# A transformer block's prelude dealt anew: the re-ordered bias rows copied by ScalarE, their transposes a later word

## The chip, the cores and the metric

The kernel runs on one core of a Trainium2 chip. The metric is the time of one execution on the device in microseconds (us). One core has TensorE (PE, its weight loads are shown as PEld), VectorE (DVE), ScalarE (ACT), GpSimd (POOL) and SyncE (SP, which here only issues transfers). Each works through its own list of instructions in order.

## The reference, cut to what matters

A PixArt-like block for 16 sequences of 256 tokens, width 256, 16 heads of 16, context of 256 tokens:

```
c_proj = silu(c) @ W_mod + b_mod          # shift_a, scale_a, gate_a, shift_m, scale_m, gate_m
x_norm = ln(x) * (1 + scale_a) + shift_a
q, k, v = split(x_norm @ W_qkv + b_qkv)
x = x + gate_a * (softmax(q k^T / 4) v @ W_proj + b_proj)
q_c = ln(x) @ W_qc + b_qc ;  k_c, v_c = split(ln(context) @ W_kvc + b_kvc)
x = x + softmax(q_c k_c^T / 4) v_c @ W_cproj + b_cproj
x = x + gate_m * (gelu((ln(x)*(1+scale_m)+shift_m) @ W_mlp1 + b_mlp1) @ W_mlp2 + b_mlp2)
```

All of it is float32; most products are done as three products of a rounded high part and a low part (hi·hi, hi·lo, lo·hi).

## The kernel before, in words

The attention work is cut into 32 units: self-attention ("s") and cross-attention ("c") of each sequence. A unit has 8 pairs of heads. While unit n is in its 8 beats (score tiles turned with the exponential, then the output product), the score maxima of unit n+1 and the projections of units n+2 and n+3 run beside it, by a written plan. Stage −1 is the 8 beats before unit 0, in which only unit 0's score maxima (its S tiles, from `s_tile`, reduced by VectorE into `mx`) are made. The MLP comes last.

Ahead of stage −1 stands the prelude, which this change deals with. Its order is a string of words, `E_['PRE']`; each word calls one function that issues instructions on one or several engines, and every engine keeps the order in which they were issued. `E_['SL']` has further words that are put behind a beat: key (−1, 3) is beat 3 of stage −1. So moving a word moves all its instructions, and its DMAs, past what other words put on the same engine.

The words that matter here:

- `load` issues the loads of x and of the first weights (wm0 and wm1 are shift_a's and scale_a's columns of W_mod, wk, wq, wv those of W_qkv; in the trace all are called wf). `lg`, `lp`, `lc`, `wm`, `ld2`, `ld3` are later loads.
- `b12`, `b5` and the like: so many zero matmuls (`busy`, wz by wz into the bank s0); each is two passes of 128x128 in the trace.
- `silu`, `turn`: silu of the condition, turned by two transposes into sT. `brow`: the bias rows (32 rows of 128) turned into columns bT, and their re-ordered copy bp, whose odd and even columns are turned as well. `scale`, `shift`: shift_a and scale_a by 16-wide products of sT with wm1, wm0 into st, then cpT by VectorE; `sc1` adds 1. `bk`, `bq`, `bv`: the biases of k, q, v, again 16-wide.
- `L0a`, `L0b`, `L0d`: layer norm of unit 0's x (statistics, rstd by GpSimd, normalising into xn); `T0t`, `T0h`, `T0l`: its transposes, high part xTh by ScalarE, low part xTl by VectorE. 1 and 2 in their place are units 1 and 2; `T2p` makes the low part by GpSimd.
- `hik`, `lok` and so on: high part (ScalarE) and low part (GpSimd, for v VectorE) of a weight.
- `K0a`, `K0m`: the two halves of unit 0's k product; `K0h`, `K0l`: its high and low part; `K0x`, `K0y`, `K0w`: the transfers of high, high again and low into big, from which the S tiles read. Q and unit 1 likewise. A `p` at the end of such a transfer's name puts it on GpSimd's queue instead of SyncE's. An S tile of a unit needs all six transfers.
- `z0kp` and so on: GpSimd fills a half of big with zeros. `vone`, `gs`, `M0`, `ga`, `pb`: ones beside v, gate products, the first turned maxima.

Of the kernel before, what the change touches and what calls it, by code (L numbers as in the profile page):

```python
# [10 lines left out]
F32 = mybir.dt.float32  # L11
# [5 lines left out]
P = 128  # L17
# [4 lines left out]
def pixart_block(  # L22
# [29 lines left out]
                return tc.keep_in_program_order(i) if self.on else i  # L52
            return issue

    E_ = {'CUT': 8, 'LN': {'s': 'pool', 'c': 'pool', 'q': 'pool'}, 'ON': (1, 1, 1), 'L0': -16, 'L1': 1, 'S0': -7, 'A0': 0, 'T0': 1, 'S1': 5, 'A1': 7, 'L2': 9, 'T1': 9, 'S2': 32, 'AP': 23, 'DV': (0, 1), 'HP': (1, 0), 'BZ': {}, 'AV': {1: [(1, 2), (1, 3)], 9: [(0, 0), (0, 1)]}, 'AHEAD': (0, 0, 0, 0, 0, 2), 'TW': {(21, 6): 'cb', (23, 5): 'u0', (23, 7): 'u1', (25, 2): 'u2', (27, 3): 'u3', (27, 7): 'h2a', (28, 0): 'l2 h0p u5', (28, 2): 'h1p', (28, 4): 'h3p', (28, 7): 'u4 u6', (29, 0): 'l3d', (29, 1): 'l0', (29, 2): 'l1', (29, 7): 'h5p', (30, 1): 'u7 h6d h7p', (30, 3): 'h4p', (31, 1): 'l4 l6d', (31, 2): 'l5d x2', (31, 4): 'l7', (31, 7): 'b2'}, 'BE': 'G0 av P g0 A1 G1 G2 N1 F7 g1 S0 PF s2 G3 aT aL p2 a2 G4 x3 b3 S1 S2 T2 C r0 G5 S3 G6 S4 s3 CF x4 F8 g2 G7 S5 F9 p3 S6 G8 a3 r1 G9 F10 G10 T3 g3 b4 S7 s4 F11 S8 S9 F12 G11 p4 a4 F13 r2 S10 G12 x5', 'XP': 1, 'IL': 1, 'MF': 0, 'SH': 4, 'RAMP': 1, 'HA': 1, 'MP': 16, 'W': (7, 1, 0, 0), 'PRE': 'z0kp load L0a z0qp L0b b12 silu hik turn lc lok one0 L0d brow ld2 scale sc1 T0t b5 L1a b1 T0h T0l z1kp L1b shift K0a bk L1d hiq K0m bq lg loq K0h hiv T1t L2a T1h K0l lp T1l Q0a K0yp K0x lov Q0m bv K1a Q0h V0a K1b Q0l K0w Q0yp Q1a Q0x Q1b Q0w K1y ld3 b7 wm V0b L2b Q1l K1l', 'SL': {(-1, 0): 'K1w z1qp L2c', (-1, 1): 'T2t one1 T2h V1a', (-1, 2): 'T2p', (-1, 3): 'z2kp K1xp ga L3a Q1yp V1b', (-1, 4): 'Q1wp pb Q1x vone M0 gs', (-1, 5): 'z2qp', (-1, 6): 'ld4 K2a L3b K2m L3p', (-1, 7): 'L3c cb lx gm', (0, 0): 'mods sp3', (0, 1): 'sp0', (0, 3): 'sp1', (0, 4): 'sc2', (0, 6): 'one2', (1, 1): 'sp2', (1, 2): 'sp4'}}

    PE = InOrder(nc.tensor, True)
    ACT, DVE, POOL, SP = (InOrder(e, True) for e in (nc.scalar, nc.vector, nc.gpsimd, nc.sync))

    const = ctx.enter_context(tc.tile_pool(name="const", bufs=1))  # L60
    work = ctx.enter_context(tc.tile_pool(name="work", bufs=2))
# [18 lines left out]
    ident = const.tile([P, P], F32, name="ident")  # L80
# [14 lines left out]
    BMOD, BQKV, BKVC, BM1 = 0, 12, 20, 24  # L95
# [13 lines left out]
    brow = const.tile([32, P], F32, name="brow")  # L109
# [31 lines left out]
    sp = [psum.tile([P, 512], F32, tag=f"s{r}", name=f"s{r}", bufs=1) for r in range(2)]  # L141
# [44 lines left out]
    def f_turn():  # L186
# [2 lines left out]
            PE.transpose(pst[:, k * B:(k + 1) * B], th[:, k * P:(k + 1) * P], ident[:B, :B])  # L189
        ACT.mul(sT.rearrange("p k b -> p (k b)"), pst[:, :KC * B], 0.5)  # L190

    def f_brow():
        pst = sp[1][:, :96]
        PE.transpose(pst[:, :32], brow, ident[:32, :32])
        ACT.copy(bT[:, 0:32], pst[:, :32])
        odd = pst[:, 32:96].rearrange("p (f r) -> p f r", f=2)
        bp = work.tile([32, 2, 2, 64], F32, tag="A", name="bp", bufs=1)
        DVE.tensor_copy(bp, brow.rearrange("r (c f) -> r f c", f=2).unsqueeze(2).to_broadcast([32, 2, 2, 64]))
        for f in range(2):
            PE.transpose(odd[:, f], bp[:, f].rearrange("r j c -> r (j c)"), ident[:32, :32])  # L200
# [87 lines left out]
    wm = []  # L288
# [9 lines left out]
    gm = []  # L298
# [19 lines left out]
    def layernorm(src, name):  # L318
# [541 lines left out]
    def mlp_T(b):  # L860
# [162 lines left out]
    u0, u1 = units[:2]  # L1023
# [4 lines left out]
    u2 = units[2]  # L1028
# [40 lines left out]
    u3 = units[3]  # L1069
# [3 lines left out]
    for i in range(5):  # L1073
        word[f"sp{i}"] = lambda i=i: f_split(i)
    word["vone"] = lambda: [POOL.memset(v[:, :, :, HD:], 1.0) for v in vts]
    for n, f in (("load", f_load), ("silu", f_silu), ("turn", f_turn), ("brow", f_brow),
                 ("scale", f_scale), ("sc1", f_sc1), ("shift", f_shift),
                 ("lg", f_loads_g), ("lp", f_loads_p), ("lc", f_loads_c), ("lx", f_loads_x),
                 ("ga", f_ga), ("pb", f_pb), ("gs", f_gs), ("cb", f_cb),
                 ("wm", f_wm), ("mods", f_mods), ("sc2", f_sc2), ("gm", f_gm)):  # L1080
        word[n] = f
    for i in range(3):
        for n, f in (("b", f_b), ("hi", f_hi), ("lo", f_lo)):
            word[n + "qkv"[i]] = lambda f=f, i=i: f(i)
# [167 lines left out]
    last, o, q = units[-1], units[-1].post, units[-2].post  # L1252
# [97 lines left out]
```

## Time and profile before

| | us |
|---|---|
| runs | 740.02, 740.80, 744.46; median 740.8 |
| profiled execution | 740.98 |
| its span, first to last instruction | 739.2 |
| TensorE busy | 728.0 (98%) |
| VectorE, ScalarE, GpSimd busy | 586.0, 555.9, 544.9 |
| mean granted TensorE clock | 0.991 of full |

In the profile a row of the timeline has: start, length, engine, line, operation, output<-inputs, shapes, count, and in brackets how long the engine stood idle ahead of it and what ended that. Every instruction has line 51, the helper that records it, so rows are told apart by their tiles. A row of a table by stretches has the stretch, its length, busy time with the number of instructions, the granted TensorE clock, the share of the DMA engines and GB/s.

### The profile page before, as it was taken

How to read it: one execution, taken by the hardware profiler on the slowest of the kernel's cores; microseconds unless marked ns; L12 is line 12 of the kernel's file. 1: busy time of each engine (PE TensorE's matmuls, PEld its weight loads, DVE VectorE, ACT ScalarE, POOL GpSimd, SP SyncE). 2: the span in 40 equal slices, each digit the busy share in tenths (PEclk: the TensorE clock that was granted, in tenths of full speed). 3: DMA queues.
4: the chain of work that ended last, by engine and by line, in shares of the span. 5: the costliest groups of instructions: out<-in, count | busy, mean ns of one | idle time of the engine just before them, and what ended most of it. 6: DMA issues, size and time to landing. Idle time of an engine off the chain costs nothing.

```text
span 739.2 us, 24891 instructions
## 1 busy us (share of the span) xinstructions
PE 728.0 (98%) x10098; PEld 643.5 (87%) x10098; DVE 586.0 (79%) x1218; ACT 555.9 (75%) x963; POOL 544.9 (74%) x572
## 2 busy tenths in 40 slices
PE   7999999999999999999999999999999999999997
PEld 7888888888888888888888888888888999999997
DVE  4778898889898898888889888888835676787872
ACT  2458888888888888888888888899886666556663
POOL 5686769778696876969687898978746767767743
PEclk8989999999999999999999999999999999999999
DMA  5653344333424334332533444344311314334221
GB/s 161 202 175 125 126 147 142 119 128 135 140 94 177 125 119 151 127 137 97 187 118 126 155 151 154 110 154 143 109 60 43 115 51 103 91 95 107 83 61 58
DMA packets 67237, 90.56 MB, mean 123 GB/s; under 512 B 6194, under 2 KB 38740, under 8 KB 67124
## 3 DMA queue, kind: packets, MB, share of 16 engines
q1 hardware_dynamic: 66452, 87.40, 35.6%
q8 instruction: 80, 1.31, 0.8%
q0 software_dynamic: 400, 1.31, 0.5%
q10 hardware_dynamic: 272, 0.26, 0.1%
q14 instruction: 33, 0.27, 0.1%
HBM read 26.97 MB, written 8.46 MB: 48 GB/s over the span
## 4 chain that ended last, share of the span: by engine, by line
PE 94%; POOL 2%; DVE 2%; ACT 1%; issue 1%; POOLq 0%; ACTq 0%
PE s L51 18%; PE o L51 16%; PE st L51 16%; PE ph L51 10%; PE ps_q L51 4%; PE ps_qc L51 4%; PE ps_kc L51 4%; PE ps_v_c L51 3%; PE ps_k L51 3%; PE ps_P_s L51 3%; PE ps_v_s L51 3%; PE ps_P_c L51 2%; PE psT_q L51 1%; PE psA_s L51 1%; PE ps_h L51 1%; PE psA_c L51 1%
## 5 line engine op out<-in xcount | busy, mean ns | idle before, releaser
L51 DVE TENSOR_REDUCE mx<-s 128x2 f32<-128x512 f32 x504 | 324.5, 683 | 65.4 <-PE s L51 59.4
L51 ACT ACTIVATE pt<-st 128x1024 f32<-128x1024 f32 x252 | 258.9, 1027 | 18.6 <-PE st L51 8.7
L51 PE MATMUL s<-big 63*128 63x256 f32 (+1 forms) x1024 | 185.8, 299 | 0.4 <-DVE mx L51 0.2
L51 PEld LDWEIGHTS s<-big 63*128 63x128 f32 (+1 forms) x1024 | 133.9, 186 | 18.9 <-DVE l_kc L51 6.6
L51 PE MATMUL st<-big 64*128 64x256 f32 (+1 forms) x1024 | 134.5, 299 | 0.0
L51 POOL TENSOR_TENSOR hl<-hf,hh 128x512 fp32r<-128x512 f32 x64 | 85.2, 1335 | 54.2 <-ACT hh L51 54.1
L51 PE MATMUL o<-pt,v 128*32 128x256 f32 x2048 | 123.8, 382 | 0.0
L51 PEld LDWEIGHTS st<-big 64*128 64x128 f32 (+1 forms) x1024 | 96.7, 186 | 15.0 <-issue 12.4
L51 PEld LDWEIGHTS o<-pt,v 128*32 128x32 f32 x2048 | 60.0, 109 | 41.5
L51 ACT ACTIVATE hf<-ph,bT 128x256 f32<-128x256 f32 x114 | 47.9, 472 | 33.7 <-PE ph L51 33.7
L51 ACT ACTIVATE hh<-ph,bT 128x256 fp32r<-128x256 f32 x114 | 47.9, 473 | 25.2 <-PE s L51 13.1
L51 ACT COPY oT<-o 128x512 f32<-128x512 f32 x63 | 36.9, 586 | 32.8 <-PE o L51 32.8
L51 PE MATMUL st<-big,hh 128*128 128x256 f32 x256 | 45.3, 277 | 0.0
L51 PE MATMUL s<-big,hh 128*128 128x256 f32 x256 | 45.2, 277 | 0.0
L51 PE MATMUL ph<-wkch,wself 128*128 128x256 f32 x224 | 44.7, 283 | 0.0
L51 PE MATMUL ph<-wqch,wself 128*128 128x256 f32 x224 | 44.6, 283 | 0.0
L51 PE MATMUL ps_k<-xTh_s,wself 64*128 64x256 f32 (+1 forms) x232 | 43.6, 293 | 0.0
L51 PE MATMUL ps_q<-xTh_s,wself 64*128 64x256 f32 (+1 forms) x240 | 41.4, 292 | 0.0
L51 POOL TENSOR_SCALAR xn_c<-c,mv_c,rs_c 128x256 f32<-128x256 f32 x32 | 38.9, 1226 | 1.7
L51 PE MATMUL ps_v_s<-wself,xTh_s 64*128 64x256 f32 x224 | 39.7, 298 | 0.0
L51 PEld LDWEIGHTS st<-big,hh 128*128 128x128 f32 x256 | 38.8, 188 | 0.0
L51 PEld LDWEIGHTS s<-big,hh 128*128 128x128 f32 x256 | 38.8, 188 | 0.0
(254 smaller groups left out, 2504.1 us busy)
## 6 DMA issues: line engine op xcount, KB each, us to landing
big<-h_kc SPq DMA_DIRECT2D x32, 256.0 KB
big<-h_qc SPq DMA_DIRECT2D x32, 256.0 KB
big<-h_k SPq DMA_DIRECT2D x30, 256.0 KB
big<-h_q SPq DMA_DIRECT2D x30, 256.0 KB
big<-l_k SPq DMA_DIRECT2D x16, 256.0 KB
g<-gd SPq DMA_DIRECT2D x16, 256.0 KB
c<-in_ctx_dram SPq DMA_DIRECT2D x16, 256.0 KB
big<-l_kc SPq DMA_DIRECT2D x16, 256.0 KB
```

The lines of the kernel that those rows point to most:

```text
L51: i = f(*a, **k)
```

## The change

The copy bp is a word of its own (`bp`) on ScalarE instead of VectorE; its transposes and what reads them are the word `bro2`, later in the prelude; the four small copies into bT become two wide ones, one on VectorE. The words of the prelude and of stage −1 are in another order. There are 28 zero matmuls instead of 25. Two transfers of unit 1 (low part of k, first copy of the high part of q) go from SyncE's to GpSimd's queue.

```diff
-'PRE': 'z0kp load L0a z0qp L0b b12 silu hik turn lc lok one0 L0d brow ld2 scale sc1 T0t b5 L1a b1 T0h T0l z1kp L1b shift K0a bk L1d hiq K0m bq lg loq K0h hiv T1t L2a T1h K0l lp T1l Q0a K0yp K0x lov Q0m bv K1a Q0h V0a K1b Q0l K0w Q0yp Q1a Q0x Q1b Q0w K1y ld3 b7 wm V0b L2b Q1l K1l',
-'SL': {(-1, 0): 'K1w z1qp L2c', (-1, 1): 'T2t one1 T2h V1a', (-1, 2): 'T2p', (-1, 3): 'z2kp K1xp ga L3a Q1yp V1b', (-1, 4): 'Q1wp pb Q1x vone M0 gs', (-1, 5): 'z2qp', (-1, 6): 'ld4 K2a L3b K2m L3p',
+'PRE': 'load L0a z0kp z0qp L0b silu b15 hik turn L0d brow bp lok T0t lg scale b5 lc sc1 ld2 L1a T0h one0 z1kp bro2 T0l hiv hiq shift K0a L1b bk K0m bq loq K0h b1 L1d K0l Q0a L2a T1t T1h lp K0yp K0x Q0m T1l bv K1a lov Q0h K0w V0a Q0l K1b Q1a L2b Q0x Q1b Q0w Q1l K1y V0b Q0yp b7 K1l ld3',
+'SL': {(-1, 0): 'wm one1 L2c z1qp', (-1, 1): 'T2t T2h V1a', (-1, 2): 'K1wp T2p', (-1, 3): 'ga K1xp L3a Q1yp V1b z2kp', (-1, 4): 'M0 Q1xp Q1wp pb L3b vone gs', (-1, 5): 'z2qp ld4', (-1, 6): 'K2a K2m L3p',
...
+    def f_bp():
+        bp = work.tile([32, 2, 2, 64], F32, tag="A", name="bp", bufs=1)
+        odd_rows.append(bp)
+        ACT.copy(bp, brow.rearrange("r (c f) -> r f c", f=2).unsqueeze(2).to_broadcast([32, 2, 2, 64]))
+
     def f_brow():
-        pst = sp[1][:, :96]
+        pst = sp[1][:, :32]
         PE.transpose(pst[:, :32], brow, ident[:32, :32])
         ACT.copy(bT[:, 0:32], pst[:, :32])
-        odd = pst[:, 32:96].rearrange("p (f r) -> p f r", f=2)
-        bp = work.tile([32, 2, 2, 64], F32, tag="A", name="bp", bufs=1)
-        DVE.tensor_copy(bp, brow.rearrange("r (c f) -> r f c", f=2).unsqueeze(2).to_broadcast([32, 2, 2, 64]))
+
+    def f_bro2():
+        odd = sp[1][:, 32:96].rearrange("p (f r) -> p f r", f=2)
         for f in range(2):
-            PE.transpose(odd[:, f], bp[:, f].rearrange("r j c -> r (j c)"), ident[:32, :32])
+            PE.transpose(odd[:, f], odd_rows[0][:, f].rearrange("r j c -> r (j c)"), ident[:32, :32])
         to = bT[:, 32:40].rearrange("p (g i f) -> p g i f", i=2, f=2)
         for par in range(2):
             rows = slice(64 * par, 64 * par + 64)
-            for g in range(2):
-                r = BQKV + 6 * g + par
-                ACT.copy(to[rows, g], odd[rows, :, r:r + 3:2].rearrange("p f i -> p i f"))
+            src = odd[rows, :, BQKV + par:BQKV + par + 12].rearrange("p f (g s) -> p g s f", g=2)
+            (DVE.tensor_copy, ACT.copy)[par](to[rows], src[:, :, 0:3:2])
```

TensorE's list at the program's start, before (s_110 and s_111 are the banks sp[0] and sp[1]; wf_112 holds wm0 and wm1):

```order
L51 MATMUL s_110<-wz 128x128 x12
L51 MATMUL st<-ident,c_sb 128x16 x2
L51 MATMUL s_111<-ident,brow 128x32
L51 MATMUL s_111<-ident,bp 128x32 x2
L51 MATMUL st<-sT,wf_112 128x16 x4
L51 MATMUL psT_s_185<-ident,xn_s_164 128x128 x4
L51 MATMUL s_110<-wz 128x128 x6
L51 MATMUL st<-sT,wf_112 128x16 x4
L51 MATMUL ps_k_217<-xTh_s_199,wself 128x256
```

And with the change:

```order
L51 MATMUL s_110<-wz 128x128 x15
L51 MATMUL st<-ident,c_sb 128x16 x2
L51 MATMUL s_111<-ident,brow 128x32
L51 MATMUL psT_s_168<-ident,xn_s_160 128x128 x4
L51 MATMUL st<-sT,wf_112 128x16 x4
L51 MATMUL s_110<-wz 128x128 x5
L51 MATMUL s_111<-ident,bp 128x32 x2
L51 MATMUL st<-sT,wf_112 128x16 x4
L51 MATMUL ps_k_217<-xTh_s_197,wself 128x256
```

The transposes of bp moved behind those of xn, the scale product and the zeros; nothing else of the head left it.

GpSimd's list from x_2's reciprocal root to the last transfer of unit 1, before (big_75 is read by unit 0's S tiles, big_76 by unit 1's):

```order
L51 DMA big_75<-h_q_301 32x4x512
L51 TENSOR_SCALAR rs_s_372<-mv_s_369 128x2
L51 TENSOR_TENSOR rs_s_372<-rs_s_372,mhalf 128x2
L51 MEMSET big_76 128x2048
L51 TENSOR_SCALAR xn_s_388<-x_177,mv_s_369,rs_s_372 128x256 x2
L51 TENSOR_TENSOR xTl_s_405<-y_s_420,xTh_s_404 128x512
L51 MEMSET big_77 128x2048
L51 DMA big_76<-h_k_317 32x4x512
L51 DMA big_76<-h_q_339 32x4x512
L51 DMA big_76<-l_q_375 32x4x512
```

And with the change:

```order
L51 TENSOR_SCALAR rs_s_335<-mv_s_332 128x2
L51 TENSOR_TENSOR rs_s_335<-rs_s_335,mhalf 128x2
L51 DMA big_75<-h_q_302 32x4x512
L51 TENSOR_SCALAR xn_s_389<-x_192,mv_s_332,rs_s_335 128x256 x2
L51 MEMSET big_76 128x2048
L51 DMA big_76<-l_k_368 32x4x512
L51 TENSOR_TENSOR xTl_s_405<-y_s_421,xTh_s_404 128x512
L51 DMA big_76<-h_k_322 32x4x512
L51 DMA big_76<-h_q_345 32x4x512
L51 MEMSET big_77 128x2048
L51 DMA big_76<-h_q_345 32x4x512
L51 DMA big_76<-l_q_349 32x4x512
```

Unit 0's second copy of h_q went behind the root, and two transfers of unit 1 came in from SyncE's list.

VectorE's list from the shift to unit 0's l_q, with the change (before, xTl of x_1 stood ahead of Wv's low part as here, but x_2's statistics stood ahead of l_k):

```order
L51 TENSOR_TENSOR cpT<-st,bT 128x32
L51 TENSOR_TENSOR bqkv<-st,bT 128x32 x2
L51 TENSOR_SCALAR xn_s_251<-x_124,mv_s_224,rs_s_227 128x256 x2
L51 SCALAR_TENSOR_TENSOR l_k_254<-ps_k_217,bqkv,h_k_247 128x256 x2
L51 SCALAR_TENSOR_TENSOR xTl_s_273<-psT_s_267,sc_103,xTh_s_272 128x256 x2
L51 TENSOR_TENSOR wself<-wf_114,wself 128x512
L51 SCALAR_TENSOR_TENSOR l_q_313<-ps_q_257,bqkv,h_q_302 128x256 x2
```

x_1's normalising now stands behind both bias sums of k and q; before it stood between them.

More of the change, by code (lines that the diff above doesn't have):

```diff
@@ L53, in __getattr__ @@
             return issue
-    E_ = {'CUT': 8, 'LN': {'s': 'pool', 'c': 'pool', 'q': 'pool'}, 'ON': (1, 1, 1), 'L0': -16, 'L1': 1, 'S0': -7, 'A0': 0, 'T0': 1, 'S1': 5, 'A1': 7, 'L2': 9, 'T1': 9, 'S2': 32, 'AP': 23, 'DV': (0, 1), 'HP': (1, 0), 'BZ': {}, 'AV': {1: [(1, 2), (1, 3)], 9: [(0, 0), (0, 1)]}, 'AHEAD': (0, 0, 0, 0, 0, 2), 'TW': {(21, 6): 'cb', (23, 5): 'u0', (23, 7): 'u1', (25, 2): 'u2', (27, 3): 'u3', (27, 7): 'h2a', (28, 0): 'l2 h0p u5', (28, 2): 'h1p', (28, 4): 'h3p', (28, 7): 'u4 u6', (29, 0): 'l3d', (29, 1): 'l0', (29, 2): 'l1', (29, 7): 'h5p', (30, 1): 'u7 h6d h7p', (30, 3): 'h4p', (31, 1): 'l4 l6d', (31, 2): 'l5d x2', (31, 4): 'l7', (31, 7): 'b2'}, 'BE': 'G0 av P g0 A1 G1 G2 N1 F7 g1 S0 PF s2 G3 aT aL p2 a2 G4 x3 b3 S1 S2 T2 C r0 G5 S3 G6 S4 s3 CF x4 F8 g2 G7 S5 F9 p3 S6 G8 a3 r1 G9 F10 G10 T3 g3 b4 S7 s4 F11 S8 S9 F12 G11 p4 a4 F13 r2 S10 G12 x5', 'XP': 1, 'IL': 1, 'MF': 0, 'SH': 4, 'RAMP': 1, 'HA': 1, 'MP': 16, 'W': (7, 1, 0, 0), 'PRE': 'z0kp load L0a z0qp L0b b12 silu hik turn lc lok one0 L0d brow ld2 scale sc1 T0t b5 L1a b1 T0h T0l z1kp L1b shift K0a bk L1d hiq K0m bq lg loq K0h hiv T1t L2a T1h K0l lp T1l Q0a K0yp K0x lov Q0m bv K1a Q0h V0a K1b Q0l K0w Q0yp Q1a Q0x Q1b Q0w K1y ld3 b7 wm V0b L2b Q1l K1l', 'SL': {(-1, 0): 'K1w z1qp L2c', (-1, 1): 'T2t one1 T2h V1a', (-1, 2): 'T2p', (-1, 3): 'z2kp K1xp ga L3a Q1yp V1b', (-1, 4): 'Q1wp pb Q1x vone M0 gs', (-1, 5): 'z2qp', (-1, 6): 'ld4 K2a L3b K2m L3p', (-1, 7): 'L3c cb lx gm', (0, 0): 'mods sp3', (0, 1): 'sp0', (0, 3): 'sp1', (0, 4): 'sc2', (0, 6): 'one2', (1, 1): 'sp2', (1, 2): 'sp4'}}
@@ new lines, in pixart_block @@
+    E_ = {'CUT': 8, 'LN': {'s': 'pool', 'c': 'pool', 'q': 'pool'}, 'ON': (1, 1, 1), 'L0': -16, 'L1': 1, 'S0': -7, 'A0': 0, 'T0': 1, 'S1': 5, 'A1': 7, 'L2': 9, 'T1': 9, 'S2': 32, 'AP': 23, 'DV': (0, 1), 'HP': (1, 0), 'BZ': {}, 'AV': {1: [(1, 2), (1, 3)], 9: [(0, 0), (0, 1)]}, 'AHEAD': (0, 0, 0, 0, 0, 2), 'TW': {(21, 6): 'cb', (23, 5): 'u0', (23, 7): 'u1', (25, 2): 'u2', (27, 3): 'u3', (27, 7): 'h2a', (28, 0): 'l2 h0p u5', (28, 2): 'h1p', (28, 4): 'h3p', (28, 7): 'u4 u6', (29, 0): 'l3d', (29, 1): 'l0', (29, 2): 'l1', (29, 7): 'h5p', (30, 1): 'u7 h6d h7p', (30, 3): 'h4p', (31, 1): 'l4 l6d', (31, 2): 'l5d x2', (31, 4): 'l7', (31, 7): 'b2'}, 'BE': 'G0 av P g0 A1 G1 G2 N1 F7 g1 S0 PF s2 G3 aT aL p2 a2 G4 x3 b3 S1 S2 T2 C r0 G5 S3 G6 S4 s3 CF x4 F8 g2 G7 S5 F9 p3 S6 G8 a3 r1 G9 F10 G10 T3 g3 b4 S7 s4 F11 S8 S9 F12 G11 p4 a4 F13 r2 S10 G12 x5', 'XP': 1, 'IL': 1, 'MF': 0, 'SH': 4, 'RAMP': 1, 'HA': 1, 'MP': 16, 'W': (7, 1, 0, 0), 'PRE': 'load L0a z0kp z0qp L0b silu b15 hik turn L0d brow bp lok T0t lg scale b5 lc sc1 ld2 L1a T0h one0 z1kp bro2 T0l hiv hiq shift K0a L1b bk K0m bq loq K0h b1 L1d K0l Q0a L2a T1t T1h lp K0yp K0x Q0m T1l bv K1a lov Q0h K0w V0a Q0l K1b Q1a L2b Q0x Q1b Q0w Q1l K1y V0b Q0yp b7 K1l ld3', 'SL': {(-1, 0): 'wm one1 L2c z1qp', (-1, 1): 'T2t T2h V1a', (-1, 2): 'K1wp T2p', (-1, 3): 'ga K1xp L3a Q1yp V1b z2kp', (-1, 4): 'M0 Q1xp Q1wp pb L3b vone gs', (-1, 5): 'z2qp ld4', (-1, 6): 'K2a K2m L3p', (-1, 7): 'L3c cb lx gm', (0, 0): 'sp3 mods', (0, 1): 'sp0', (0, 3): 'sp1', (0, 4): 'sc2', (0, 6): 'one2', (1, 1): 'sp2', (1, 2): 'sp4'}}
@@ L190, in f_turn @@
         ACT.mul(sT.rearrange("p k b -> p (k b)"), pst[:, :KC * B], 0.5)
+    odd_rows = []
+    def f_bp():
+        bp = work.tile([32, 2, 2, 64], F32, tag="A", name="bp", bufs=1)
+        odd_rows.append(bp)
+        ACT.copy(bp, brow.rearrange("r (c f) -> r f c", f=2).unsqueeze(2).to_broadcast([32, 2, 2, 64]))
     def f_brow():
-        pst = sp[1][:, :96]
+        pst = sp[1][:, :32]
         PE.transpose(pst[:, :32], brow, ident[:32, :32])
         ACT.copy(bT[:, 0:32], pst[:, :32])
-        odd = pst[:, 32:96].rearrange("p (f r) -> p f r", f=2)
-        bp = work.tile([32, 2, 2, 64], F32, tag="A", name="bp", bufs=1)
-        DVE.tensor_copy(bp, brow.rearrange("r (c f) -> r f c", f=2).unsqueeze(2).to_broadcast([32, 2, 2, 64]))
+    def f_bro2():
+        odd = sp[1][:, 32:96].rearrange("p (f r) -> p f r", f=2)
         for f in range(2):
-            PE.transpose(odd[:, f], bp[:, f].rearrange("r j c -> r (j c)"), ident[:32, :32])
+            PE.transpose(odd[:, f], odd_rows[0][:, f].rearrange("r j c -> r (j c)"), ident[:32, :32])
         to = bT[:, 32:40].rearrange("p (g i f) -> p g i f", i=2, f=2)
@@ L1075, in pixart_block @@
     word["vone"] = lambda: [POOL.memset(v[:, :, :, HD:], 1.0) for v in vts]
-    for n, f in (("load", f_load), ("silu", f_silu), ("turn", f_turn), ("brow", f_brow),
+    for n, f in (("load", f_load), ("silu", f_silu), ("turn", f_turn), ("brow", f_brow), ("bp", f_bp), ("bro2", f_bro2),
                  ("scale", f_scale), ("sc1", f_sc1), ("shift", f_shift),
```

## The prediction

> **What bounds the kernel now.** I read the page first: its head, its row of granted clock and the shares of the chain that ended last.
>
> ```profile
> span 739.2 us, 24891 instructions
> PE 728.0 (98%) x10098; PEld 643.5 (87%) x10098; DVE 586.0 (79%) x1218; ACT 555.9 (75%) x963; POOL 544.9 (74%) x572
> PEclk8989999999999999999999999999999999999999
> PE 94%; POOL 2%; DVE 2%; ACT 1%; issue 1%; POOLq 0%; ACTq 0%
> ```
>
> TensorE is the bound: 98% busy, 94% of the chain. What lies off TensorE is in the prelude and at the very end, and the clock is below full speed only in the first slice (18.5 us each) and the third. The change touches only what happens before about 45 us; everything later issues in the same order, so whatever the prelude gives or takes should pass through to the end unchanged. The next view is the timeline of all engines around TensorE's hole.
>
> ```profile
> 6.48 0.73 DVE L51 TENSOR_SCALAR xn_s<-x,mv_s,rs_s 128x256 f32<-128x256 f32 x2 [1.43 <-POOL rs_s L51]
> 6.95 1.41 POOL L51 TENSOR_TENSOR wself<-wf,wself 128x512 fp32r<-128x512 f32 x1 [0.51 <-ACT wself L51]
> 7.13 3.11 DVE L51 COPY bp<-brow 32x256 f32<-32x256 f32 x1
> 8.30 1.80 POOL L51 MEMSET big<- 128x2048 f32 x1
> 10.39 0.39 PE L51 MATMUL s<-ident,bp 32*128 32x32 f32 x2 [3.63 <-DVE bp L51]
> 10.82 0.44 ACT L51 COPY bT<-s 64x4 f32<-64x4 f32 x4 [3.79 <-PE s L51]
> ```
>
> TensorE stands 3.63 us for one small copy on VectorE, and everything behind its two transposes stands too, though xn_s was ready at 7.21. The copy of 32x256 lasts 3.11 us and ends 0.14 us after GpSimd's memset (10.10). The hole has a second price, in the granted clock (columns: stretch, its length, busy PE with its instructions, clock, DMA share, GB/s; the last row has PE, PEld, DVE, ACT and POOL):
>
> ```profile
> 9.00:10.00 1.00, 0.00 (x0) 0.84 1.04 334
> 10.00:11.00 1.00, 0.61 (x4) 0.50 0.73 216
> 16.00:17.00 1.00, 1.00 (x9) 0.75 0.00 0
> 17.00:18.00 1.00, 1.00 (x11) 1.00 0.00 0
> 43.50:44.00 0.50, 0.50 (x9) 0.81 0.98 338
> 44.00:44.50 0.50, 0.50 (x6) 0.50 0.91 311
> 50.50:51.00 0.50, 0.50 (x11) 0.86 0.00 0
> 29.00:41.00 12.00, 11.78 (x83) 7.49 (x85) 11.72 (x21) 3.83 (x9) 9.62 (x12) 1.00 0.63 201
> ```
>
> From about 9.7 to 16.5 TensorE runs at half clock, 6.8 us, and again from 43.7 to 50.6, 6.9 us. The work there is on the path:
>
> ```profile
> 1.04 5.42 PE L51 MATMUL s<-wz 128*128 128x128 f32 x24 [1.04 <-DVE wz L51]
> 10.71 1.89 PE L51 MATMUL st<-sT,wf 128*128 128x16 f32 x8
> 12.44 1.09 PE L51 MATMUL psT_s<-ident,xn_s 128*128 128x128 f32 x4
> 13.33 2.77 PE L51 MATMUL s<-wz 128*128 128x128 f32 x12
> 15.89 1.26 PE L51 MATMUL st<-sT,wf 128*128 128x16 f32 x8
> 17.00 0.36 PE L51 MATMUL ps_k<-xTh_s,wself 128*128 128x256 f32 x1
> 22.15 0.96 PE L51 MATMUL st<-cpT,wf 128*128 128x16 f32 x8
> 26.52 1.73 PE L51 MATMUL s<-wz 128*128 128x128 f32 x14
> 28.88 0.50 PE L51 MATMUL st<-big 63*128 63x256 f32 x4
> 40.64 0.38 PE L51 MATMUL s<-big 63*128 63x256 f32 x1
> ```
>
> The same zero matmul takes 0.226 us a pass in the first stretch (5.42/24), 0.231 at 13.33 and 0.124 at 26.52, so the first stretch is half speed as well, although its row of clock reads 1.00 until the first event. The first K product starts at 17.00, the first S tile of unit 0 at 28.88 and the first of unit 1 at 40.64. TensorE is without a gap from 10.39 to 28.88, so the first two are set by its program, not by operands.
>
> **The change part by part.** *The copy of bp goes to ScalarE.* No row shows it there. Lower bound: ScalarE's activation of 256 elements on 16 partitions, 0.41 us below; upper bound: the 3.11 us that it took on VectorE, if the strided reading is slow by itself. I take 0.41: 3.11 us would be 12 ns an element, and no other row is near that.
>
> The Trainium skill, SBUF — State Buffer, section "Who interferes with whom", says that a copy on VectorE in its two-port mode and a GpSimd instruction exclude each other for the whole instruction. The rows agree as far as the copy ends with the memset; by the rule the price on ScalarE is the lower bound.
>
> *Transposes of bp a word later.* In TensorE's queue they now stand behind xn's transposes, the scale product and ten zero passes, so they no longer hold anything up.
>
> The rows for the new head:
>
> ```profile
> 3.12 0.41 ACT L51 ACTIVATE c_sb<-c_sb 16x256 f32<-16x256 f32 x1 [0.41 <-DMA c_sb<-in_cond_dram]
> 6.78 0.19 ACT L51 ACTIVATE sT<-st 128x32 f32<-128x32 f32 x1
> 9.87 0.33 SPq L51 DMA_DIRECT2D gb<-in_L_xcond_b_mod_dram  x1
> 12.71 0.19 DVE L51 TENSOR_TENSOR cpT<-st,bT 128x32 f32<-128x32 f32 x1 [2.47 <-PE st L51]
> 12.94 0.18 DVE L51 TENSOR_SCALAR sc<-cpT 128x32 f32<-128x32 f32 x1
> 13.57 0.84 ACT L51 ACTIVATE xTh_s<-psT_s,sc 128x256 fp32r<-128x256 f32 x2 [2.31 <-PE psT_s L51]
> 14.45 0.88 DVE L51 SCALAR_TENSOR_TENSOR xTl_s<-psT_s,sc,xTh_s 128x256 fp32r<-128x256 f32 x2 [0.67 <-ACT xTh_s L51]
> ```
>
> Thirty zero passes instead of 24: at 0.226 they end at 1.04 + 6.8 = 7.8; if the clock rises on the way, the six added cost 0.7, so 7.0 to 7.2. I take 7.4. Two transposes of cond and one of brow, 0.4 as before: 7.8. xn's transposes (at full clock half of 1.09): 8.4. sT on ScalarE is ready at 8.1, so the scale product, 8 passes at the 0.96 of 22.15, ends at 9.3. VectorE: cpT and sc, 0.19 + 0.18 with their latencies: 9.75. ScalarE's xTh, 0.84: 10.6. VectorE meanwhile takes x_1's statistics, which it cannot start before x_1 lands: the SyncE row at 9.87 is the issue that waits for that landing, so 9.9 to 10.6. Ten zero passes at 0.124 (1.2) end at 10.5, bp's transposes at 10.8 (their operand since 8.7), VectorE's half of the bT copy at 11.0, xTl at 11.9 with its first half at 11.5. The shift product ends at 11.65. **The first K product starts at about 11.7 instead of 17.00: 5.3 us earlier.** If the bp copy costs 3.11, xTh starts at 11.4 instead of 9.75 and this shrinks to 3.6.
>
> *From there to the first S tile* TensorE's list needs 28.88 − 17.00 = 11.9 us, plus two zero passes (0.2): 23.8. Two waits that the hole had hidden come up, because VectorE's list does not shrink: xTl of x_1, which VectorE now takes after l_k and x_2's statistics, and Wv's lower part, together about 0.6. So 24.4. Of the moved transfers the one that could bind is the second copy of h_q, which GpSimd now issues behind x_2's reciprocal root:
>
> ```profile
> 23.50 0.56 POOL L51 DMA_DIRECT2D big<-h_q  x1 [1.91 <-ACT h_q L51]
> 24.62 0.22 POOL L51 TENSOR_SCALAR rs_s<-mv_s 128x2 f32<-128x2 f32 x1 [0.56 <-DVE mv_s L51]
> 24.92 0.72 POOL L51 TENSOR_TENSOR rs_s<-rs_s,mhalf 128x2 f32<-128x2 f32 x1
> 36.27 0.55 POOL L51 DMA_DIRECT2D big<-l_q  x1
> big<-h_q POOLq DMA_DIRECT2D x2, 256.0 KB, 3.1
> ```
>
> Statistics ready at 24.5 − 4.4 = 20.1, root until 21.1, issue, landing 3.1 later: 24.2, just inside 24.4. **First S tile 24.4 instead of 28.88: 4.5 earlier.**
>
> *The last transfers of unit 1.* l_k and the first copy of h_q leave SyncE's queue for GpSimd's, two more issues of 0.55. GpSimd's chain to the last of them, counted from 21.7 with xTl (T2) waiting until 27.6, is at 32.4; the l_q issue at 36.27 landed by the 40.64 of the old S tile, and with 3.5 us to land (3.1 for h_q) the new one is at 35.9 against 40.64 − 4.5 = 36.1. I charge 0.1 for it. What is queued behind these issues on GpSimd is the ones of v and gb's product, neither due before unit 0's output products (some 15 us later), so they cost nothing; without that cover they would cost 1.1.
>
> The rest (two wide bT copies for four small ones, wga ahead of wcp on SyncE, the wide zero words, one bank's statistics earlier) lies under TensorE's list or is part of the count above.
>
> Sum: 4.5 − 0.1 = **4.4 us**. The profiled execution took 740.98 us (span 739.2), 0.2 above the median 740.8; 740.98 − 4.4 = 736.6, and by the median 736.4. I forecast **736.5**.
>
> **The rivals.**
>
> *The clock falls in the new prelude all the same.* The fall at 43.7 came while PE was 100% busy in the rows, after a stretch of 16-wide and half-array matmuls. The new list puts the scale and shift products, bp's transposes and 0.3 us of waiting between 8.4 and 11.7, with only 1.2 us of zeros among them. Against it: from 17 to 18 the old list mixes 16-wide and full products and holds 1.00. One fall is 6.8 us at half speed, 3.4 us of work, of which the waits above (0.6) absorb some: 736.5 + 2.9 = 739.4.
>
> The Trainium skill, TensorE: Matmul & The Clock Gate, section "What's actually happening", has half clock only after an idle window of about 3.4 us; by that rule this rival is nothing, and the fall at 43.7, with no idle at all, speaks against the rule.
>
> *The second fall goes too.* The sparse stretch before 43.7 is moved by 4.4 us against whatever counts activity; if it is cut otherwise, unit 0 keeps full clock and wins another 3.0 or so (3.4 less what VectorE then bounds): 733.5. Against it: nothing in that stretch is made denser.
>
> *The GpSimd queue is late.* Its chain to unit 1's last transfer has 0.2 us to spare by the count above and five issues in it. If each of them, or the landing of the last, is held up by 0.4 us, the first S tile of unit 1 waits 2 us: 738.5. The Trainium skill, SBUF — State Buffer, section "SBUF: two separate sides", warns that a DMA issued by GpSimd cannot write its descriptors while VectorE runs a two-port copy. The issues in the two rows above took 0.55 and 0.56.
>
> *Slower.* The clock falls in the prelude and once more in unit 0's S stage (24 to 36), which already consists of 63-row products that wait for VectorE. It decides once more than 4.4 us of TensorE's work is lost, so with two falls: 736.5 + 6.8 = 743.3. Against it: the old S stage, the same list, holds 1.00 from 29 to 41.
>
> **How the numbers follow.** Forecast (3.3 to 5.8 us gained) 0.58; clock falls in the prelude 0.18; second fall gone 0.10; GpSimd late, or bp dear on ScalarE (737.5 to 738.5), 0.10; slower 0.04. Range: from the second-fall case to the prelude-fall case with half a microsecond beyond, **733.4 to 740.4**, leaving out slightly over one in ten. A measurement of this kernel tells about 1%, 7.4 us, from no change: faster than 733.4 needs the second fall gone and a little luck, 0.06; slower than 748.2 needs three falls, 0.02; within 1%, 0.92.
>
> **What would show it.** Right: no idle of TensorE on bp; clock 1.00 from about 7 to the first S tile; the first K product at 11.5 to 12.0, the first S tile at 24 to 25, unit 1's at 36 to 36.7; the bp copy on ScalarE near 0.4. Wrong: a granted clock of 0.50 between 10 and 24, an S tile that waits for a GpSimd transfer by over 1 us, or a later stage that gives back what the prelude won: then the claim that the rest only shifts has failed.

## The result and the profile after

Over 22 runs each on one chip the changed kernel took 736.48 us (median; 733.89 to 741.39) and the kernel before 740.9 (735.03 to 747.39): a ratio of 0.9941, 95% interval 0.9918 to 0.9964. On a second chip (first experiment) the gain was not told from nothing. The forecast was 736.5. The number came out; the way to it did so only in part. Two runs of the kernel before on the fourth chip used, 964 and 1146 us at a clock of 0.65 and 0.62, are left out everywhere below.

The page of the profiled execution of the changed kernel, which took 738.99 us, more than its median:

```profile
span 737.1 us, 24900 instructions
PE 728.8 (99%) x10104; PEld 643.6 (87%) x10104; DVE 583.4 (79%) x1218; ACT 556.2 (75%) x961; POOL 546.9 (74%) x574
PEclk8899999999999999999999999999999999999999
PE 95%; DVE 2%; POOL 1%; ACT 1%; issue 1%; POOLq 0%; ACTq 0%; DVEq 0%
```

The third slice is back at full clock, the second is below it. The timeline of TensorE answers to the rows of before:

```profile
7.71 1.06 PE L51 MATMUL st<-sT,wf 128*128 128x16 f32 x8
8.63 1.36 PE L51 MATMUL s<-wz 128*128 128x128 f32 x10
9.92 0.31 PE L51 MATMUL s<-ident,bp 32*128 32x32 f32 x2
11.34 0.38 PE L51 MATMUL ps_k<-xTh_s,wself 128*128 128x256 f32 x1
12.22 0.58 PE L51 MATMUL ps_k<-xTl_s,wself 128*128 128x256 f32 x1 [0.50 <-DVE xTl_s L51]
29.24 0.50 PE L51 MATMUL st<-big 63*128 63x256 f32 x4
40.99 0.38 PE L51 MATMUL s<-big 63*128 63x256 f32 x1
```

No idle on bp is left and the first K product is 5.7 us earlier. Yet the first S tile, at 29.24, is later than before (28.88). The stretches show why (length; busy PE, PEld, DVE, ACT, POOL with counts; granted clock; DMA share; GB/s):

```profile
12.00:13.00 1.00, 0.78 (x3) 0.78 (x4) 0.81 (x5) 1.00 (x2) 0.10 (x1) 0.61 0.53 179
13.00:14.00 1.00, 1.00 (x8) 1.00 (x6) 0.00 (x0) 0.04 (x1) 0.92 (x3) 0.50 0.00 0
22.00:23.00 1.00, 1.00 (x9) 1.00 (x8) 0.70 (x2) 0.77 (x2) 0.00 (x0) 0.77 0.00 0
40.00:50.00 10.00, 9.88 (x115) 8.50 (x117) 8.25 (x17) 5.96 (x10) 9.43 (x11) 1.00 0.55 188
```

From about 12.2 to 22.5 (a microsecond at 0.61 holds 0.78 us of half clock) TensorE runs at half clock. The second fall, 43.8 to 50.6 before, is gone in this execution: 1.00 all through. The other engines:

```profile
7.62 0.42 ACT L51 COPY bp<-brow 32x256 f32<-32x256 f32 x1
8.88 1.80 POOL L51 MEMSET big<- 128x2048 f32 x1
9.11 1.60 DVE L51 TENSOR_SCALAR sc<-cpT 128x32 f32<-128x32 f32 x1
36.88 0.55 POOL L51 DMA_DIRECT2D big<-l_q  x1
```

The copy of bp took 0.42 us on ScalarE. But sc, costed at its old 0.18, took 1.60 and ended at 10.71, with GpSimd's memset (10.68): the hold that had sat on VectorE's copy now sat on the next instruction of that kind. (In the record the statistics of x_1 and the copy into bT behind sc start inside its 1.60 us, at 9.49 and 10.26, and end with it at 10.71; ScalarE's xTh, which reads sc, starts at 10.81.)

### The profile page after: what moved, and what is told of

Same layout as the page of the kernel before. It is cut to its first block, busy times and chain, and to the rows that moved or that the text cites. A ratio compares the mean times of both kernels' runs of the same rounds, so it can differ in the third digit from the quotient of the medians.

```text
span 737.1 us, 24900 instructions
## 1 busy us (share of the span) xinstructions
PE 728.8 (99%) x10104; PEld 643.6 (87%) x10104; DVE 583.4 (79%) x1218; ACT 556.2 (75%) x961; POOL 546.9 (74%) x574
## 4 chain that ended last, share of the span: by engine, by line
PE 95%; DVE 2%; POOL 1%; ACT 1%; issue 1%; POOLq 0%; ACTq 0%; DVEq 0%
PE s L51 18%; PE o L51 16%; PE st L51 16%; PE ph L51 11%; PE ps_qc L51 5%; PE ps_q L51 5%; PE ps_kc L51 4%; PE ps_k L51 3%; PE ps_v_c L51 3%; PE ps_P_s L51 3%; PE ps_v_s L51 3%; PE ps_P_c L51 2%; PE ps_h L51 1%; PE psT_q L51 1%; PE psA_c L51 1%; PE psA_s L51 1%
```

## The experiments

Medians are of one set of runs on one chip, the ratio is to the kernel before on the same chip. Lengths at half clock are worked out as above. First, both kernels once more as they are. **The changed kernel again**, on a second chip:

> The changed kernel itself, for the runs of this chip and their granted clocks. Theory C (the gain is mostly clock): in the changed kernel's runs the time follows the mean granted clock, about 734 us at 1.000 and about 739 us at 0.992, and runs without any fall occur; median near 736.5. Rival H (the gain is the hole alone, 3.6 us of idle): the runs with full clock and those without lie 4 us below the kernel before alike, and the clock does not sort them.

737.48 us (734.52 to 741.65, 12 runs) against 737.72 (734.34 to 747.14, 35 runs): ratio 0.9987 [0.9958, 1.0015]. sc took 1.61 us again, the clock was at half from 12.7 to 26.3 and 46.8 to 50.2, the first S tile came at 30.57. The hold on sc came both times; how much clock was lost differed.

**The kernel before again** (one profile, on a fourth chip):

> The kernel before itself, for another profile of it. Theory L (a race decides the hole): if the high part of wk is ready on ScalarE after about 7.0, VectorE's bp copy starts first and takes 0.3 us, TensorE's wait for it is 0 to 1 us, GpSimd's subtraction starts behind it; if it is ready before, the copy takes over 3 us as in the first profile. Rival (the hole is in every execution): 3.1 us whatever the landing.

739.31 us. The rows that answer to the hole of the first profile:

```profile
6.45 0.66 ACT L51 CAST wself<-wf 128x512 fp32r<-128x512 f32 x1 [3.45 <-DMA wf<-in_L_xcond_W_qkv_dram]
7.13 0.27 DVE L51 COPY bp<-brow 32x256 f32<-32x256 f32 x1
7.18 1.38 POOL L51 TENSOR_TENSOR wself<-wf,wself 128x512 fp32r<-128x512 f32 x1 [0.74 <-ACT wself L51]
7.55 0.28 PE L51 MATMUL s<-ident,bp 32*128 32x32 f32 x2 [0.84 <-DVE bp L51]
9.16 1.19 DVE L51 TENSOR_SCALAR sc<-cpT 128x32 f32<-128x32 f32 x1
11.00:23.00 12.00, 12.00 (x59) 12.00 (x59) 5.16 (x16) 3.46 (x9) 3.00 (x4) 0.50 0.29 94
29.51 0.50 PE L51 MATMUL st<-big 63*128 63x256 f32 x4
```

The same copy at the same place took 0.27 us instead of 3.11. In the first profile GpSimd's subtraction started at 6.95, 0.18 ahead of the copy; here wk's load landed 0.23 later (cast at 6.45 against 6.22), the subtraction started at 7.18, 0.05 behind the copy, and the copy was not held. So the hole of 3.63 us is the outcome of a race, and as far as these two profiles show the load decides it. sc met the memset (8.51 to 10.31) here too and took 1.19. The time is nearly as long all the same, for the clock was at half from 9.6 to 23.2, though TensorE is without a gap from 7.55 on.

**Only the engine of the copy.** The changed kernel with the copy back on VectorE, and the kernel before with its copy on ScalarE, all else as it was:

```diff
# changed kernel
-        ACT.copy(bp, brow...)
+        DVE.tensor_copy(bp, brow...)
# kernel before
-        DVE.tensor_copy(bp, brow...)
+        ACT.copy(bp, brow...)
```

> The changed kernel with the bp copy back on VectorE, all else as changed. Theory L (the copy was long only because GpSimd held a shared resource with its subtraction and memset): it now starts at 7.2 while GpSimd still waits for the high part of wk until about 7.6, so it takes 0.2 to 0.5 us, nothing behind it is late, and the time stays within 0.5 us of the changed kernel. Rival I (the strided copy is slow on VectorE by itself): it takes 3.1 us again, the scale sum cpT comes at 10.3 instead of 8.9, and the first K product is 1.4 us later: 1 to 1.5 us slower than the changed kernel.

> The kernel before with the bp copy alone moved to ScalarE, no word moved. Theory: TensorE's 3.63 us hole shrinks to under 1 us, the first K product comes at 13 to 14.5, and sc on VectorE now meets GpSimd's memset and ends with it, as in the changed kernel. By theory C the time is 736 to 738 with most of the whole gain; by the rival that the new order of words carries the gain, it stays at 739 to 741.

The first took 737.3 us, ratio 0.9973 [0.9939, 1.0007], the second 739.48, ratio 0.9997 [0.9964, 1.0031]. The copy in the first:

```profile
7.15 0.28 DVE L51 COPY bp<-brow 32x256 f32<-32x256 f32 x1
9.30 1.06 DVE L51 TENSOR_SCALAR sc<-cpT 128x32 f32<-128x32 f32 x1
```

0.28 us: the strided copy is not slow by itself. And in the second:

```profile
7.45 0.41 ACT L51 COPY bp<-brow 32x256 f32<-32x256 f32 x1
7.92 0.30 PE L51 MATMUL s<-ident,bp 32*128 32x32 f32 x2 [1.44 <-ACT bp L51]
```

On ScalarE it took 0.41, TensorE still waited 1.44 for it, and the gain that was expected of it did not come. The engine of the copy alone is worth nothing that these runs can tell. On this chip they could not tell the whole change from nothing either (0.9987), so they say only that the copy is not a large part of it. Of the other parts the order of the words and the zeros are tried below; the two transfers of unit 1 and the two wide bT copies are not tried by themselves.

**The memset behind the low part of Wq**, out of sc's way:

```diff
-T0h one0 z1kp bro2 T0l hiv hiq shift K0a L1b bk K0m bq loq K0h b1
+T0h one0 bro2 T0l hiv hiq shift K0a L1b bk K0m bq loq z1kp K0h b1
```

> The changed kernel with GpSimd's zero fill of unit 1's half of big moved behind Wq's low part, all else as changed. Theory L: sc on VectorE takes 0.2 us instead of 1.60, xTh starts at 9.4 instead of 10.8, TensorE's wait for xTl (0.50, and 0.9 us of late products) is gone, the clock falls less often; 0.5 to 1.5 us faster than the changed kernel. Rival: sc's 1.60 us has another cause (its operand cpT or the statistics of x_1 beside it) and stays; time unchanged within 0.5 us.

735.87 us (734.09 to 737.06), ratio 0.993 [0.9901, 0.9959], on the chip where the changed kernel had 0.9987.

```profile
9.09 0.18 DVE L51 TENSOR_SCALAR sc<-cpT 128x32 f32<-128x32 f32 x1
11.05 0.36 PE L51 MATMUL ps_k<-xTh_s,wself 128*128 128x256 f32 x1
24.40 0.50 PE L51 MATMUL st<-big 63*128 63x256 f32 x4
36.14 0.38 PE L51 MATMUL s<-big 63*128 63x256 f32 x1
14.64 1.53 DVE L51 TENSOR_SCALAR xn_s<-x,mv_s,rs_s 128x256 f32<-128x256 f32 x2
15.91 0.86 PE L51 MATMUL psT_s<-ident,xn_s 128*128 128x128 f32 x4 [0.40 <-DVE xn_s L51]
8.00:24.00 16.00, 15.53 (x129) 14.78 (x129) 8.96 (x29) 6.77 (x17) 9.18 (x11) 1.00 0.59 201
40.00:46.00 6.00, 6.00 (x55) 6.00 (x56) 3.29 (x6) 3.47 (x5) 5.28 (x8) 0.50 0.45 161
```

sc is back at 0.18, the prelude holds 1.00, and the S tiles stand where the prediction had put them, 24.4 and 36.1. The memset, at 13.91 now, has a new victim, though: the normalising of x_1 takes 1.53 us instead of 0.73, and TensorE waits 0.40 for it. One fall is left, 39.8 to 46.7. Run again on the fourth chip:

> The kernel of e4 once more, on this chip beside the three others: mean 735.2 to 736.2, fastest near 734.1, no run below a mean clock of 0.994, and 3 to 4 us below the kernel before in the mean. If e4's result was luck of the chip, the mean lies at 737 to 738 like the changed kernel's in e1.

735.28 us (734.08 to 736.65), ratio 0.9946 [0.9919, 0.9973]. This profile has no fall at all:

```profile
24.34 0.50 PE L51 MATMUL st<-big 63*128 63x256 f32 x4
8.00:24.00 16.00, 15.52 (x128) 14.79 (x128) 8.98 (x29) 6.74 (x16) 9.01 (x11) 1.00 0.60 204
24.00:60.00 36.00, 35.63 (x406) 28.28 (x404) 32.15 (x61) 20.69 (x35) 30.59 (x36) 1.00 0.55 181
```

Of all versions tried this one has the lowest medians, on both chips.

**The same memset move in the kernel before**, which takes its hold away without the new order:

```diff
-b1 T0h T0l z1kp L1b shift K0a bk L1d hiq K0m bq lg loq K0h
+b1 T0h T0l L1b shift K0a bk L1d hiq K0m bq lg loq z1kp K0h
```

> The kernel before with one word moved: GpSimd's zero fill of unit 1's half of big goes behind Wq's low part, as in e4; the bp copy stays on VectorE in its old place. Theory L+C: the copy can be held only by GpSimd's subtraction, so it ends by 8.5 at the latest, the hole is at most 1.9 us and only where wk lands early; falls of the clock in the prelude get rare; mean of the runs 735.5 to 737 against the kernel before's 739.45, that is as much as the whole change brings. Rival (the new order of the words carries the gain): the mean stays within 1 us of 739.45.

740.08 us, ratio 1.0015 [0.9979, 1.0051].

```profile
7.14 0.28 DVE L51 COPY bp<-brow 32x256 f32<-32x256 f32 x1
9.44 0.18 DVE L51 TENSOR_SCALAR sc<-cpT 128x32 f32<-128x32 f32 x1
10.00:23.00 13.00, 13.00 (x64) 13.00 (x63) 5.43 (x17) 3.38 (x9) 4.74 (x5) 0.50 0.33 110
29.77 0.50 PE L51 MATMUL st<-big 63*128 63x256 f32 x4
```

Neither the copy nor sc is held, and the clock still falls from 9.8 to 23.4. The theory had expected 735.5 to 737, so it missed: these holds are not what costs the old order its clock.

**Fewer zeros, and more.** The memset-later version without its `b5` and `b1` (12 passes); the kernel before with the memset later and three zero matmuls more at the start and five behind `scale` (16 passes):

```diff
# changed kernel, memset later
-scale b5 lc sc1    K0h b1 L1d
+scale lc sc1       K0h L1d
# kernel before, memset later
-L0b b12 silu       scale sc1
+L0b b15 silu       scale b5 sc1
```

> The kernel of e4 without the zero matmuls b5 and b1 (six of its 28), which change nothing in the output. Theory C (zeros keep the clock up between the 16-wide products): without them TensorE stands 1 us ahead of the first K product, the clock falls in the prelude in half of the runs or more, and the mean rises from 735.6 by 0.5 to 2. Rival (they are only work): nothing falls, the first S tile comes up to 0.4 us earlier, mean 735.2 to 735.6.

> The kernel of e6 (before, zero fill later) with b12 made b15 and five zero matmuls more behind the scale product, as the changed kernel has them; nothing else. Theory C (what the change gave is density in the first 13 us): falls in the prelude go, the mean drops from 739.9 to 736 or 737. Rival (the order of the other words matters): it stays at 739 or above.

Fewer: 737.98 us (735.92 to 741.43), ratio 0.9994 [0.9958, 1.003], the mean 2.4 us above that of the same order with its zeros (738.03 against 735.62, on another chip), and no run above a clock of 0.994. More: 737.6 (735.77 to 741.36), ratio 0.9979 [0.9952, 1.0006], between theory and rival: the mean is 1.5 us below that of the memset move alone (738.33 against 739.88, on another chip), but the intervals of the two ratios overlap. Of these two in turn:

```profile
13.00:24.00 11.00, 11.00 (x57) 11.00 (x57) 4.88 (x15) 2.66 (x7) 4.99 (x7) 0.54 0.33 121
27.29 0.50 PE L51 MATMUL st<-big 63*128 63x256 f32 x4
```

```profile
17.00:20.00 3.00, 2.89 (x13) 2.76 (x14) 2.67 (x9) 0.84 (x2) 0.66 (x1) 0.50 0.47 175
27.26 0.50 PE L51 MATMUL st<-big 63*128 63x256 f32 x4
```

Taking 1.5 us of zero matmuls out (12 passes at 0.124) brought back about 10 us of half clock, and putting some into the old order cut it from 13.6 us to 3.4, in one profile each. Without these zeros none of 12 runs has a mean clock above 0.994, with them none of 23 lies below it: in the new order the zeros do carry the clock. They do not do it alone: on the fourth chip the old order with its 33 zeros has a mean of 738.33, the new one with 28 has 735.23.

**What stands before the second fall.** The memset-later version with the 16-wide `mods` products three beats later; then the same with the memset behind `K0yp` (from `T1h lp K0yp K0x` to `T1h lp K0yp z1kp K0x`) instead of `loq`; then the memset-later version with mods in place and ten zero matmuls about them:

```diff
# mods later, in both of the first two
-(0, 0): 'sp3 mods',      (0, 3): 'sp1'
+(0, 0): 'sp3',           (0, 3): 'sp1 mods'
# zeros about mods
-(-1, 7): 'L3c cb lx gm',     (0, 0): 'sp3 mods'
+(-1, 7): 'L3c cb lx gm d4',  (0, 0): 'sp3 mods d6'
```

> The kernel of e4 with the word mods (16 products 16 wide) moved from beat 0 to beat 3 of unit 0, so that it no longer follows the other sparse products of stage -1's end. Theory M (the second fall of the clock is set off by that sparse stretch): the fall at about 40 to 47 becomes rare, the group of runs at a mean clock of 0.994 shrinks, mean of the runs 734.3 to 735.0 against e4's 735.6. Rival (the fall comes from S and t tiles on half the array, whatever stands between them): the groups stay, mean 735.3 to 736.

> The changed kernel with the zero fill moved one word further than in e4, behind the first of unit 0's k transfers that GpSimd issues, and mods moved as in e5. In e4 the fill, at 13.91, met xn of x_1 on VectorE (1.22 us for its first half instead of 0.4) and TensorE stood 0.40 us for it. Theory L: that wait goes too, the first S tile comes at 23.8 to 24.2 instead of 24.40, mean 0.3 us below e5. Rival: xn is held by something else and the S tile stays at 24.4.

> The kernel of e4 with ten more zero matmuls (four at the end of stage -1, six behind mods), which change nothing in the output; 20 passes cost about 2.2 us of TensorE. Theory C (dense passes hold the clock): no fall near 40 any more, no run at a mean clock of 0.995, all runs within 1 us of each other at 736 to 736.7. Rival (the fall there is not one of density): the groups stay as in e4 and all come 2.2 us later, 736.3 to 739.2.

Mods later: 736.6 us, ratio 0.9976 [0.9947, 1.0005]; the fall stood at 39.2 to 46.0 all the same, and the best run was 1.2 us longer (735.29 against 734.09, on another chip): the theory that mods bring the fall is out. The memset behind `K0yp` was to free x_1's normalising, which the last move had caught: 740.84 us, ratio 1.0018 [0.9987, 1.0049], the mean 3.5 us above that of mods later alone (740.19 against 736.65, same chip). The new place was a worse one:

```profile
14.63 2.98 DVE L51 TENSOR_SCALAR xn_s<-x,mv_s,rs_s 128x256 f32<-128x256 f32 x2
15.64 1.82 POOL L51 MEMSET big<- 128x2048 f32 x1
17.67 0.55 PE L51 MATMUL psT_s<-ident,xn_s 128*128 128x128 f32 x3 [2.06 <-DVE xn_s L51]
```

The normalising of x_1 took 2.98 us (x_0's took 0.73 in the profile of before); the first half took 0.40 as ever, the second 2.67: it began at about 14.95, while GpSimd was issuing a transfer (14.83 to 15.63), and ended just behind the memset (17.61 and 17.46). TensorE waited 2.06 for it. Zeros about mods: 736.71 us, ratio 0.9967 [0.9949, 0.9984], and all 12 runs within 736.55 to 737.77 at a clock of 0.999 or more.

```profile
8.00:26.00 18.00, 17.20 (x143) 16.26 (x143) 10.14 (x32) 6.82 (x17) 9.47 (x12) 1.00 0.56 191
26.00:60.00 34.00, 33.64 (x356) 26.31 (x355) 29.02 (x54) 17.92 (x30) 27.71 (x33) 1.00 0.50 164
```

The fall can be kept away in every run, at 2.5 us for the zeros (736.55 against 734.08 for the best runs), which is more than the falls cost there (mean 736.85 against 735.23 without these zeros, on the same chip).

## Why the prediction was right, and where it was not

The profiles together answer the claim on which the sum rests, that **the rest only shifts**. The falls are worked out from stretches of half a microsecond at their ends; the last column is the span less the start of the first S tile. The three kernels edited behind the S tile (mods later, zeros about mods) are left out:

| profile | half clock before the S tile, us | first S tile | half clock after it, us | rest |
|---|---|---|---|---|
| before | 6.8 | 28.88 | 6.8 | 710.3 |
| before again | 13.6 | 29.51 | none | 708.0 |
| before, copy on ScalarE | 3.4 | 25.23 | 6.8 | 710.9 |
| before, memset later | 13.6 | 29.77 | none | 708.2 |
| before, memset later, more zeros | 3.4 | 27.26 | none | 708.1 |
| changed | 10.2 | 29.24 | none | 707.9 |
| changed again | 13.6 | 30.57 | 3.4 | 709.2 |
| changed, copy on VectorE | 6.8 | 27.38 | none | 708.1 |
| changed, memset later | none | 24.40 | 6.8 | 710.5 |
| the same, fewer zeros | 10.2 | 27.29 | 3.4 | 709.2 |
| changed, memset later, again | none | 24.34 | none | 707.9 |

The rest is 707.9 to 708.2 without a later fall, 709.2 with one of 3.4 us, 710.3 to 710.9 with one of about 6.8, whichever the order. So the claim held: what is won ahead of the first S tile comes out at the end, and the rest varies with the clock alone. A later fall costs about 0.36 of its length (2.5 of 6.8 us), one ahead of the S tile about 0.46 (6.2 of 13.6, the hold on sc included).

**The first K product** was forecast at 11.7 and came at 11.34. The wait for bp was gone, and the copy took 0.42, the lower bound, as chosen. But two errors stood against each other here:

```profile
1.04 5.67 PE L51 MATMUL s<-wz 128*128 128x128 f32 x30 [1.04 <-DVE wz L51]
10.81 0.84 ACT L51 ACTIVATE xTh_s<-psT_s,sc 128x256 fp32r<-128x256 f32 x2 [2.77 <-DVE bT L51]
```

The first zeros ended at 6.71, not at 7.4, and all that TensorE had behind them was 0.4 to 0.7 us early; sc came 0.96 late (10.71 for 9.75). So the product waited for xTh and not for TensorE's own list, as the forecast had it, and its second part waited 0.50 for xTl. Without the hold on sc it came at 11.05 and 10.92.

**The failed step is the first S tile**, and it failed in two terms. *sc at 0.18.* The row of before had it right only because it came after the memset; in the new order it starts 0.23 us behind the memset's start and ends 0.03 us behind its end. The Trainium skill, SBUF — State Buffer, section "Who interferes with whom", counts tensor_scalar with copy among the operations that can contend with GpSimd, where the one that issues first blocks the other for its whole instruction. Both traces agree (1.60 and 1.61 us ending with the memset; 0.18 with the memset elsewhere); the prediction had applied it to the copy alone. *The clock.* The forecast had 1.00 up to the S tile and gave a fall there 0.18, at 6.8 us; it was 10.2 and 13.6. That is 4.8 and 6.2 us on the S tile, as measured against the 24.4 that came where the clock held, the hold on sc included. The sign named for this, 0.50 between 10 and 24, is what the profile shows, so in that execution the forecast's way had failed; it lost the prelude's clock, as one rival had it, and won the second fall back, as another had it. That 24.4 itself came out with the memset moved is luck in part: the first K product was 0.65 and 0.78 us ahead of its forecast, and the stretch from there to the S tile took 13.35 and 13.42 us where 12.7 had been counted, 0.40 of it the wait for x_1's normalising that the moved memset brings.

**The base was mis-sized as well.** The hole of 3.63 us was costed as if every execution had it. It is a race between VectorE's copy and GpSimd's subtraction, and all four later profiles with the copy on VectorE (the kernel before, its two versions with the memset later, the changed kernel with the copy back) show the other outcome, 0.27 to 0.28 us. How often it falls which way in runs without a profile is not known. At one mean clock, 0.991, the runs of the kernel before lie in two groups, eight at 738.7 to 739.5 and five at 741.0 to 741.4, and the first profile (740.98) belongs with the second; that the hole makes the second group is not shown.

Two small slips change nothing: the second fall of before began at 43.8 (the row at 0.81 holds 0.19 us of half clock) and lasted 6.8, and "half a microsecond beyond" the two cases of the range gives 733.0 to 739.9.

**Why the number came out all the same.** Runs with the same clock take nearly the same time in both kernels; what differs is how many runs fall into each group. The kernel before is counted on the second to fourth chip, where the clock of each of its runs is listed, the changed one on the first and second, the version with the memset later on the second and fourth:

| mean granted clock | before, 97 runs | changed, 34 runs | changed, memset later, 23 runs |
|---|---|---|---|
| 0.996 and more | 14 (733.7 to 735.6) | 10 (733.9 to 735.9) | 16 (734.1 to 736.5) |
| 0.993 to 0.995 | 29 (736.8 to 738.3) | 15 (736.1 to 737.6) | 7 (736.4 to 737.1) |
| 0.989 to 0.992 | 19 (738.7 to 741.4) | 6 (739.0 to 740.1) | none |
| below | 35 (740.7 to 747.1) | 3 (741.1 to 741.7) | none |

The columns are of different chips. On the second chip alone the kernel before has 5, 14, 2 and 14 runs in the four groups, the changed one 3, 4, 4 and 1, the version with the memset later 7, 5, none and none. So there the changed kernel's mix is hardly a better one, and that of the last version is.

With its clock whole the old order is no longer than the new: 733.69 at best against 733.89, and 733.61 with the copy on ScalarE, though only three of the 97 runs of the kernel before got there (0.999 and more). An estimate says the same: its S tiles less half the falls stand at 22.7 (29.51 − 6.8) and 23.5 (25.23 − 1.7), ahead of 24.4, and at 25.5 (28.88 − 3.4) in the profile with the hole. So at full clock nothing was won by the 4.4 us of the sum; what the change brings, where it brings something, is fewer and shorter falls, and it takes both the new order and its zeros, as the versions with the memset later show. The median moved by 4.4 us on one chip and by 0.2 on another, since the mix of runs differs by chip (the kernel before: 737.72, 738.66, 739.62 and 740.9 on four). That the median met 736.5 within 0.1 is partly chance.

**The other terms.** GpSimd's queue was not late: its last transfer of unit 1 was issued at 36.88 and unit 1's S tile did not wait for it. With the hold gone, that S tile stood at 36.14 against a forecast of 36.1. The rival "slower" did not come up in the medians.

**Still open:** what exactly sets a fall. They last 3.41, 6.83, 10.24 and 13.65 us, whole steps of 3.41. In the clock records of the twelve profiles with a fall, the first one begins a whole number of such steps behind the clock's first rise (9.68 − 6.27 and 12.22 − 5.39), and that rise lies anywhere from 5.1 to 6.6 us. So the steps stand otherwise to the program in each execution, which may be why the same program shows a fall in one and none in another (40 to 46 in the memset-later version); it is not shown. The step ahead of a fall reads, in the kernel before with the memset later and in the kernel before:

```profile
6.35:9.76 3.41, 2.41 (x21) 2.17 (x21) 1.44 (x6) 1.30 (x8) 1.40 (x2) 1.00 1.05 343
40.40:43.81 3.41, 3.41 (x36) 3.03 (x35) 2.91 (x8) 1.29 (x2) 3.13 (x5) 1.00 0.80 228
```

In all ten profiles with a fall ahead of the S tile, TensorE stood idle for some of the step before it, 0.25 us (changed, copy on VectorE) to 2.92 (before). Such waits may set these falls off, but they are not enough: the memset-later version waits 0.40 for x_1's normalising and keeps its clock. Five of the six later falls follow a step without any idle time. What is counted over a step, no run isolates. Nor is it shown why the mix differs by chip.

## What to carry to other kernels

Before a stall is costed, compare the starts of the two instructions that collide: where they lie within a few tenths and one hangs on a load, the stall is a race, and one profile shows one outcome of it. Read the clock of every run before the medians; if runs at one clock agree between two kernels, it is the clock that the change acts on, and a dense filler in a sparse stretch is worth its own time only where falls cost more (here 1.5 us in the prelude paid, 2.5 us about mods did not). When a hold is removed by moving one victim, look which instruction of the same kind issues next under the same holder; when the holder is moved instead, look what it meets at its new place (one place here cost 0.40 us of waiting and paid, the next cost 2.06 and did not).

## What the hardware showed unexpectedly

- Half clock goes on for 10 to 13 us with TensorE at 100% in the rows, in stretches with many 16-wide products (13.00 us busy of 13.00 at 0.50), and can begin so as well: 3.41 of 3.41 us busy ahead of the fall at 43.8.
- A memset of GpSimd, which only writes, holds a 128x32 operation of VectorE that starts 0.23 us behind it until its own end: 1.60 us instead of 0.18. One of xn that started while GpSimd issued a transfer took 2.67 instead of 0.40 and ended with the memset behind that issue.
- The same copy took 3.11 us where it started 0.18 us behind GpSimd's subtraction, and 0.27 where it started 0.05 ahead of it.
- With enough zeros, twelve runs lie within 1.2 us of each other (736.55 to 737.77), where 25 of the 27 runs of the kernel before on the same chip spread over 9.5.
